# Two cross-attention layers on one core: who writes the second copy of the fifth head group

## The chip, the core and the metric

One core of a Trainium2 chip runs the whole program. The metric is device time in microseconds, the median of several executions. TensorE (PE) multiplies matrices, VectorE (DVE) and ScalarE (ACT) work element by element and can read PSUM, where TensorE puts its results, GpSimd (POOL) works in SBUF, and SyncE (SP) issues most transfers (DMA).

## The reference

Two layers of cross-attention, one behind the other, on 16 sequences of 256 rows with 320 channels, 20 heads of 16 channels each. The context has 256 rows of 512. Its first rows are text (77 in layer 0, 252 in layer 1), the others image tokens (layer 1: the last 4). Shortened, layer 1:

```python
q = heads(hidden_states @ W_q)
k_t, v_t = heads(text_ehs @ W_k), heads(text_ehs @ W_v)
probs_t = softmax(einsum('bhsd,bhtd->bhst', q, k_t) * attn_scale)
text_out = einsum('bhst,bhtd->bhsd', probs_t, v_t)
...
fused = attn_scores + SEM_SCALE * sem
probs_ip = softmax(fused) * spatial_mask[None, None, :, None]
out = text_out + IP_SCALE * einsum('bhsn,bhnd->bhsd', probs_ip, v_ip)
out = out @ W_out + b_out + residual
```

Layer 0 has the same form with another semantic term (`sem` comes from unsplit queries and is shared by all heads) and its own token counts.

## The kernel before

The work is cut into batches b = 0 to 15 and, within each batch, five groups g = 0 to 4 of four heads. A group of one layer is a slot; slot k = 5b + g, 80 slots in layer 0 (`NS`), 80 in layer 1. Each slot forms scores (into PSUM), their row maxima, the exponentials (tile `P`, in SBUF), the products with the values, and then settles them: `settle0` (line 804) or `settle1` (line 985).

**Settling.** The products of a group come with the softmax's denominator as a 17th column, heads along the partitions. VectorE transposes them in blocks of 32x32 (line 807 or 991), takes the reciprocal of the denominator into an unused part of the same PSUM bank (`rz`, line 810 or 1000) and multiplies.

- Layer 0: text and image parts each have a denominator, so VectorE multiplies both (line 813, tile `tmp`, 128x256) and GpSimd adds the two halves into `hsn` (line 814, 128x128).
- Layer 1: VectorE multiplies once, straight into `hsn` (line 1001, 128x128).

**The tile `hsn`** is [128, 3, 8, 2, 16]: three blocks p, 8 row groups, two head groups r, 16 channels. Group g goes to block g // 2, place g % 2. Five groups fill two and a half blocks, and the second place of the third block is filled with a second copy of group 4: it is there so that the output projection's third block can be used for a high and a low part of the same numbers. That copy is made by GpSimd: line 816 in layer 0, line 1005 in layer 1, 128x128 each, once per batch.

**Behind it.** `gather` (line 819) has VectorE transpose the three blocks of `hsn` into `hT` (line 826, 128x256 each); there is one `hsn` and one `hT` for all batches. `finish` (line 830) splits `hT` into high and low parts (`split`, line 589: ScalarE at 593 and 594, GpSimd at 595 and 596) and projects them (TensorE, line 606 and 609). In layer 1, line 1060 (VectorE) adds the image part to `hT` before the split.

**Other work of the same queues.** GpSimd: the multiplies of line 769 in layer 0 and the subtractions of line 925 in layer 1 (128x512, four per slot), splits of context and queries (163, 595, 596), small casts of line 529, which wait for a transfer, the image softmax of layer 1 (1017 to 1050, with the power at 1022). VectorE: the reductions of 740, 741 and 894, which read the scores, the products of line 935, and most PSUM evacuation.

**Order.** Generators are advanced by due times given in slots (`task`, `fill`, `later`; `gather` becomes due 0.45 or 0.4 slots after the fifth group is settled). That gives the program order. In the main loop only TensorE keeps it exactly:

```python
with tc.manual_schedule(engines=PINNED):
    for k in range(2 * NS + 2):
```

`PINNED` holds PE alone, and the context is opened with `schedule_with_timeline_sim=True` (line 1301): a planner sorts the instructions of the other engines at build, by durations that it assumes, and puts in the waits. In the prologue (`begin`) all engines keep the written order. A few instructions are tied behind others of their engine (`anchor`, `queued`).

Of the kernel before, what the change touches and what calls it, by code (L numbers as in the profile page):

```python
# [30 lines left out]
NG = H // 4  # L31
# [18 lines left out]
def xattn2(  # L50
# [27 lines left out]
    nc = tc.nc  # L78
# [31 lines left out]
    def buf(tag, shape, dtype=F32, bufs=1, name=None):  # L110
        if tag in ("wB", "wD", "vr", "raw"):
            return sb.tile(shape, dtype, tag=tag, name=name or tag, bufs=bufs)
        size = 1
        for d in shape[1:]:
            size *= d
        if tag not in slots:
            slots[tag] = [0, dtype] + [const_tile([128, max(size, words.get(tag, 0))], f"{tag}_{i}", dtype) for i in range(bufs)]
        n, kind, *ring = slots[tag]
        assert kind == dtype and len(ring) == bufs, tag
        slots[tag][0] += 1  # L120
        t = ring[n % bufs][: shape[0], :size]
        names = "abcd"[: len(shape) - 1]
        if len(names) > 1:
            t = t.rearrange(f"p ({' '.join(names)}) -> p {' '.join(names)}", **dict(zip(names, shape[1:])))
        return t
# [645 lines left out]
    def attend0(k):  # L771
        b, g = divmod(k, NG)
        v, pv = get("v0", b), own("P")
        for vt in range(3):
            values0(k, pv, v, vt)
        settle0(b, g, pv)
# [27 lines left out]
    def settle0(b, g, pv):  # L804
        hn = hsn
        nt = buf("nt", [128, 2, 8, 32], bufs=2)
        nc.vector.transpose(nt.rearrange("p a f c -> p (a f c)"), pv)  # L807

        rz = pv[:, :16].rearrange("p (a f) -> p a f", a=2)
        nc.vector.reciprocal(rz, nt[:, :, :, 16])  # L810
        nc.vector.tensor_mul(rz[:, 1], rz[:, 1], mk)
        tmp = buf("tmp", [128, 2, 8, 16], bufs=2)
        nc.vector.tensor_mul(tmp, nt[:, :, :, 0:16], rz.unsqueeze(3).to_broadcast([128, 2, 8, 16]))
        nc.gpsimd.tensor_add(hn[:, g // 2, :, g % 2], tmp[:, 0], tmp[:, 1])
        if g == NG - 1:
            nc.gpsimd.tensor_copy(hn[:, 2, :, 1], hn[:, 2, :, 0])
            later(0.45, lambda: gather(0, b))

    def gather(l, b):

        n = l * B + b - 1
        while n >= 0 and ("taken", n) not in results:
            step((f"c{n // B}", n % B))
        hT = buf("hT", [128, 3, S])
        for p in range(3):
            nc.vector.transpose(hT[:, p], hsn[:, p].rearrange("p f r d -> p (f r d)"))
        results["gathered", l, b] = hT
        return hT
# [108 lines left out]
    def attend1(k):  # L937
        pv = bank("P")
        ours, before = k < 2 * NS, k > NS
        if ours:  # L940
            b, g = divmod(k - NS, NG)
            v = get("t1", b)[0]
            for n in range(2):
                for s in range(4):
                    h = V1W * (4 * g + s)
                    mm(  # L946
                        pv[32 * s : 32 * s + 32, :S],
                        v[:, n, h : h + 32],
                        P[k, s // 2][:, n, s % 2],
                        start=n == 0,  # L950
                        stop=n == 1 and not before,
                    )
        if before:
            for n in range(2):
                for s in range(4):
                    mm(pv[32 * s : 32 * s + 32, :S], zone, W[k - 1, s // 2][:, n, s % 2], start=n == 0 and not ours, stop=n == 1)  # L956
        settle1(k, pv)
# [27 lines left out]
    def settle1(k, pv):  # L985
        hn = hsn
        b, g = divmod(k - NS, NG)
        if "na" not in w1:
            w1["na"] = buf("nt", [128, 2, 8, 32], bufs=2, name="na")
        na = w1["na"][:, (k - NS) % 2]  # L990
        nc.vector.transpose(na.rearrange("p f c -> p (f c)"), pv[:, :S])
        if g == 0 and b:
            nc.gpsimd.tensor_copy(norms[b - 1][:, NG, :, 5], na[:, :, 21])
        if b == B:
            return
        if g == 0:
            norms[b] = buf("tmp", [128, NG + 1, 8, 6], bufs=2, name="n1")
        nc.gpsimd.tensor_copy(norms[b][:, g], na[:, :, 16:22])
        rz = pv[:, S : S + 8]
        nc.vector.reciprocal(rz, na[:, :, 16])  # L1000
        nc.vector.tensor_mul(
            hn[:, g // 2, :, g % 2], na[:, :, 0:16], rz.unsqueeze(2).to_broadcast([128, 8, 16])
        )
        if g == NG - 1:
            nc.gpsimd.tensor_copy(hn[:, 2, :, 1], hn[:, 2, :, 0])
            later(0.4, lambda: gather(1, b))

    def image_softmax(b, lo=0, hi=NG):
# [99 lines left out]
    def later(slots, make):  # L1108
        delayed.append((clock[0] + slots, make))
# [196 lines left out]
```

## Time and profile before

| what | value |
|---|---|
| median of 3 runs | 1557.14 us (1554.51 to 1558.83) |
| profiled execution | 1557.65 us |
| its span, first to last instruction | 1555.9 us |
| mean granted TensorE clock | 0.97 |
| layer 0 / layer 1 border | about 751 us |

The profile's page gives busy time per engine over the whole span. Since the two layers have different limits, the views to use are those by window. A row of the groups by line reads: line, engine, operation, output <- inputs, shape, count, then busy time and mean duration of one, then the engine's idle time before it and what ended it. The chain of waits follows the work that ended last back from the end; a piece on it is start, length, engine, tile and line.

### The profile page before, as it was taken

The page shows a single profiled execution, that of the slowest core. Times are in us where ns is not written, and L with a number is a line of the kernel's source. Part 1 is how long each engine was busy: PE and PEld are TensorE (multiplying, and loading weights), DVE is VectorE, ACT ScalarE, POOL GpSimd, SP SyncE. Part 2 cuts the span into 40 slices and gives each one's busy share as a digit, 9 for nine tenths or more (in the row PEclk, how much of TensorE's full clock was granted, in tenths as well). Part 3 has the DMA queues.
Part 4 walks back from the last instruction along what each step waited for, and adds up shares of the span by engine and source line. Part 5 has one row for each costly group of instructions (what it writes and reads, how often), then busy time and mean ns, then how long its engine had stood idle before and what let it go on. Part 6 is the DMA issues. An engine that isn't in the chain of part 4 may idle for free.

```text
span 1555.9 us, 35997 instructions
## 1 busy us (share of the span) xinstructions
PE 1453.4 (93%) x12726; PEld 1169.1 (75%) x12726; DVE 1119.9 (72%) x2544; ACT 891.6 (57%) x2037; POOL 1266.6 (81%) x1357
## 2 busy tenths in 40 slices
PE   6789899989998988888999999999999999999996
PEld 5678787878786877666777777777777778777764
DVE  5466667657666686886777777777778777778784
ACT  5345465645555544554666666666666666666562
POOL 4159698978898886797778988889888988889797
PEclk9899899999999998899999999999999999999998
DMA  6766667666767575666453444444443444433411
GB/s 210 193 185 174 183 183 223 187 205 168 227 168 236 147 222 153 185 179 175 134 158 90 140 112 114 130 119 118 123 134 109 143 110 118 134 114 97 120 32 36
DMA packets 228815, 233.04 MB, mean 150 GB/s; under 512 B 38410, under 2 KB 198508, under 8 KB 228620
## 3 DMA queue, kind: packets, MB, share of 16 engines
q1 hardware_dynamic: 226428, 229.44, 51.8%
q8 instruction: 101, 1.65, 0.5%
q10 hardware_dynamic: 2208, 1.30, 0.3%
q14 instruction: 78, 0.64, 0.1%
HBM read 118.04 MB, written 77.10 MB: 125 GB/s over the span
## 4 chain that ended last, share of the span: by engine, by line
PE 62%; POOL 15%; DMA 8%; DVE 6%; ACT 4%; issue 3%; SPq 2%; ACTq 1%; DVEq 0%; POOLq 0%
PE X L934 13%; PE X L248 12%; PE X L606 6%; POOL wt L925 5%; PE P L796 5%; PE P L946 4%; PE S L739 4%; POOL P L769 4%; PE P L956 3%; PE T L763 3%; PE S L892 3%; PE T L886 3%; DMA qs<-qd 2%; PE X L258 2%; SPq L83 2%
## 5 line engine op out<-in xcount | busy, mean ns | idle before, releaser
L769 POOL TENSOR_TENSOR P<-P,rs 128x512 f32<-128x512 f32 x320 | 408.0, 1299 | 118.0 <-ACT P L766 117.0
L925 POOL TENSOR_TENSOR wt<-P,ctb 128x512 f32<-128x512 f32 x320 | 405.5, 1292 | 61.5 <-ACT ctb L924 61.5
L934 PE MATMUL X<-ctb,gm 128*128 128x512 f32 x1120 | 304.9, 401 | 0.1
L766 ACT ACTIVATE P<-T 128x512 f32<-128x512 f32 x320 | 175.7, 594 | 162.1 <-PE T L763 131.4
L935 DVE TENSOR_TENSOR wt<-X,wt 128x512 f32<-128x512 f32 x320 | 216.9, 683 | 35.3 <-PE X L934 26.8
L934 PEld LDWEIGHTS X<-ctb,gm 128*128 128x128 f32 x1120 | 195.9, 189 | 31.1 <-DVE wt L935 0.6
L906 ACT ACTIVATE P<-T 128x512 f32<-128x512 f32 x320 | 173.6, 595 | 77.5 <-PE T L886 74.6
L924 ACT ACTIVATE ctb<-P 128x512 fp32r<-128x512 f32 x320 | 187.9, 627 | 23.9 <-PE X L934 20.5
L894 DVE TENSOR_REDUCE mn<-S 128x4 fp32r<-128x1008 f32 x160 | 191.6, 1198 | 0.0
L741 DVE TENSOR_REDUCE mn<-S 128x4 fp32r<-128x716 f32 x160 | 142.7, 892 | 0.0
L796 PE MATMUL P<-P,vr 128*32 128x256 f32 x1920 | 132.7, 408 | 5.4 <-POOL P L769 3.5
L739 PE MATMUL S<-ks,qs 125*128 125x256 f32 x640 | 120.8, 313 | 8.2 <-DMA qs<-tph 5.2
L739 PEld LDWEIGHTS S<-ks,qs 125*128 125x128 f32 x640 | 91.2, 200 | 45.8 <-issue 28.4
L763 PE MATMUL T<-qs,ks 127*128 127x256 f32 x640 | 110.6, 295 | 3.4 <-DMA qs<-mt 2.0
L1022 POOL TENSOR_TENSOR r<-u,rs 128x40 f32<-128x40 f32 (+2 forms) x17 | 108.7, 6395 | 4.4 <-DVE u L1019 4.4
L740 DVE TENSOR_REDUCE mn<-S 128x4 fp32r<-128x308 f32 x160 | 74.7, 467 | 33.7 <-PE S L739 32.6
L763 PEld LDWEIGHTS T<-qs,ks 127*128 127x128 f32 x640 | 93.1, 199 | 6.5 <-ACT P L766 2.6
L807 DVE STREAM_TRANSPOSE nt<-P 128x512 f32<-128x512 f32 x80 | 57.1, 714 | 55.5 <-PE P L796 54.9
L796 PEld LDWEIGHTS P<-P,vr 128*32 128x32 f32 x1920 | 57.6, 114 | 49.8 <-issue 10.6
L606 PE MATMUL X<-ho,wF 128*128 128x256 f32 x512 | 75.7, 289 | 19.3 <-POOL ho L596 11.1
L606 PE MATMUL X<-hq,wE 128*128 128x256 f32 x512 | 82.3, 301 | 11.1 <-POOL hq L595 5.8
L606 PEld LDWEIGHTS X<-ho,wF 128*128 128x128 f32 x512 | 67.1, 190 | 28.7 <-POOL ho L596 12.1
(234 smaller groups left out, 3042.7 us busy)
## 6 DMA issues: line engine op xcount, KB each, us to landing
qd<-q SPq DMA_DIRECT2D x96, 256.0 KB
qs<-tph SPq DMA_DIRECT2D x64, 308.0 KB
rawc<-in_cT_dram SPq DMA_DIRECT2D x60, 256.0 KB
qs<-qd SPq DMA_DIRECT2D x80, 192.0 KB
ks<-kd SPq DMA_DIRECT2D x80, 192.0 KB
ks<-kd SPq DMA_DIRECT2D x160, 96.0 KB
qs<-qd SPq DMA_DIRECT2D x160, 96.0 KB
kd<-kst SPq DMA_DIRECT2D x57, 256.0 KB
```

The costliest lines, as they stand in the source:

```text
L248: last = mm(out, lhs(a, k), rhs(b, k), start=i == 0, stop=i == len(terms) - 1)
L606: mm(pp, w(s, k, m), a[:, t], start=i == 0, stop=i == len(terms) - 1)
L739: mm(sp[:, h], Q[: XROW + T0, h, t * 128 : (t + 1) * 128], K[: XROW + T0, h], start=True, stop=True)
L763: mm(st[p][:, j], K[:KS0, 2 * p + j, t * 128 : (t + 1) * 128], Q[:KS0, 2 * p + j], start=True, stop=True)
L766: exp = anchor(nc.scalar.activation(pt, st[p], AF.Exp, scale=SCALE))
L769: anchor(nc.gpsimd.tensor_mul(pt, pt, rs[:, t : t + 1].to_broadcast([128, 2, S])))
L796: mm(pv[32 * s : 32 * s + 32, o : o + S], v[:, vt, h : h + 32], P[k, s // 2][:, t, s % 2], start=vt < 2, stop=vt != 1,)
L894: anchor(nc.vector.tensor_reduce(maxes[k + 2][:, t], sp[:, :, :T1], axis=AX.X, op=ALU.max))
L924: nc.scalar.activation(R[k, u][:, t], P[k, u][:, t], AF.Copy, scale=0.5)
L925: anchor(nc.gpsimd.tensor_sub(W[k, u][:, t], P[k, u][:, t], f(R[k, u][:, t])))
L934: mm(yp, gm[:, gb], R[k, u][:, kt], start=i == 0, stop=i == len(blocks[n]) - 1)
L935: nc.vector.tensor_mul(W[k, u][:, n], yp, W[k, u][:, n])
```

## The change

In both layers the fifth group (g = 4) is written to both places of the third block by one instruction. The inputs are read twice by an access pattern that repeats the 16 channels (a broadcast over the place r), so that the output is the whole block, 128x256 and contiguous. The two GpSimd copies go. Groups 0 to 3 stay as they were.

```diff
-        nc.gpsimd.tensor_add(hn[:, g // 2, :, g % 2], tmp[:, 0], tmp[:, 1])
-        if g == NG - 1:
-            nc.gpsimd.tensor_copy(hn[:, 2, :, 1], hn[:, 2, :, 0])
+        if g < NG - 1:
+            nc.gpsimd.tensor_add(hn[:, g // 2, :, g % 2], tmp[:, 0], tmp[:, 1])
+        else:
+            one, two = [tmp[:, i].unsqueeze(2).to_broadcast([128, 8, 2, 16]) for i in range(2)]
+            nc.gpsimd.tensor_add(hn[:, 2], one, two)
             later(0.45, lambda: gather(0, b))
...
-        nc.vector.tensor_mul(
-            hn[:, g // 2, :, g % 2], na[:, :, 0:16], rz.unsqueeze(2).to_broadcast([128, 8, 16])
-        )
-        if g == NG - 1:
-            nc.gpsimd.tensor_copy(hn[:, 2, :, 1], hn[:, 2, :, 0])
+        if g < NG - 1:
+            nc.vector.tensor_mul(
+                hn[:, g // 2, :, g % 2], na[:, :, 0:16], rz.unsqueeze(2).to_broadcast([128, 8, 16])
+            )
+        else:
+            one, two = [t.to_broadcast([128, 8, 2, 16]) for t in (na[:, :, 0:16].unsqueeze(2), rz.unsqueeze(2).unsqueeze(3))]
+            nc.vector.tensor_mul(hn[:, 2], one, two)
             later(0.4, lambda: gather(1, b))
```

In layer 0 the work stays on GpSimd, in layer 1 the second half moves from GpSimd to VectorE, and the third transpose of line 826 then follows its producer on the same engine.

## The prediction

> **What bounds the kernel now.** I read the page's totals first, then the busy time of each engine in windows cut at the stage borders (layer 0 up to about 751 us, layer 1 behind it, the last batch from 1490).
>
> ```profile
> span 1555.9 us, 35997 instructions
> PE 1453.4 (93%) x12726; PEld 1169.1 (75%) x12726; DVE 1119.9 (72%) x2544; ACT 891.6 (57%) x2037; POOL 1266.6 (81%) x1357
> core 0: us, PE busy (x) PEld busy (x) DVE busy (x) ACT busy (x) POOL busy (x), PEclk, DMA share, GB/s
> 206.00:528.00 322.00, 303.11 (x2806) 257.28 (x2803) 215.48 (x522) 179.80 (x432) 277.34 (x277) 0.98 0.68 197
> 528.00:751.00 223.00, 195.66 (x1704) 159.07 (x1703) 168.39 (x373) 118.44 (x281) 181.37 (x191) 0.92 0.64 181
> 755.00:1150.00 395.00, 390.94 (x3454) 304.49 (x3454) 306.45 (x669) 250.68 (x554) 333.14 (x376) 1.00 0.44 122
> 1150.00:1490.00 340.00, 338.13 (x3021) 262.14 (x3020) 266.60 (x585) 215.35 (x473) 299.81 (x326) 1.00 0.41 116
> 1490.00:1556.00 66.00, 51.04 (x389) 35.41 (x387) 40.16 (x87) 24.66 (x48) 51.41 (x57) 0.91 0.12 37
> ```
>
> The reader is to see two different kernels. In layer 1 TensorE is idle for 4.06 us of 395 and 1.87 us of 340, at a granted clock of 1.00: whatever VectorE or GpSimd saves there meets an engine that hardly waits. In layer 0 TensorE is idle for 18.9 us of 322 and 27.3 us of 223, and in the last 66 us for 15.0 us; there GpSimd, VectorE, ScalarE and transfers take turns on the path, so there an order can gain or lose. GpSimd is busiest after TensorE, 81% of the span, and the change is mostly about its queue.
>
> **The rows of the changed work**, from the groups by line with shapes kept apart (the last columns are busy us, mean ns of one, idle before).
>
> ```profile
> L814 POOL TENSOR_TENSOR hsn<-tmp 128x128 f32<-128x128 f32 x80 | 37.8, 472 | 3.7 <-DVE tmp L813 3.7
> L816 POOL COPY hsn<-hsn 128x128 f32<-128x128 f32 x16 | 4.7, 296 | 0.0
> L1005 POOL COPY hsn<-hsn 128x128 f32<-128x128 f32 x16 | 4.7, 291 | 0.0
> L998 POOL COPY tmp<-nt 128x48 f32<-128x48 f32 x80 | 18.1, 226 | 2.4 <-DVE nt L991 2.4
> L596 POOL TENSOR_TENSOR ho<-hT,ho 128x256 fp32r<-128x256 f32 x32 | 23.6, 737 | 2.5 <-ACT ho L594 2.5
> L1050 POOL TENSOR_TENSOR rs<-rs,kb 128x384 f32<-128x384 f32 x16 | 16.3, 1018 | 0.0
> L1001 DVE TENSOR_TENSOR hsn<-nt,P 128x128 f32<-128x128 f32 x80 | 22.9, 286 | 2.3
> L813 DVE TENSOR_TENSOR tmp<-nt,P 128x256 f32<-128x256 f32 x80 | 33.3, 416 | 2.0
> L935 DVE TENSOR_TENSOR wt<-X,wt 128x512 f32<-128x512 f32 x320 | 216.9, 683 | 35.3 <-PE X L934 26.8 <-POOL wt L925 4.2
> L163 DVE TENSOR_TENSOR wB<-rawc,wB 128x512 fp32r<-128x512 f32 x3 | 4.0, 1335 | 0.0
> ```
>
> **Layer 0, GpSimd.** One copy per batch goes: 16 of 296 ns, 4.7 us. The add of the fifth group grows from 128 to 256 elements a partition, 16 times. The trace has no such add; the nearest row, the 128x256 add at line 596, takes 737 ns. Bounds: 472 ns, if the second read of the same 16 values costs nothing, and 1018 ns, the 128x384 row. I take 740, so 16 x (740 - 472) = 4.3 us come back, net -0.4 us of GpSimd work, between -4.7 and +4.0. No DMA, no queue and no other engine's instruction is moved by the text of the change. The third transpose (line 826, VectorE) waited for the copy and will wait for the longer add.
>
> [...]
>
> From the rows: the copy costs (291 - 226) / 80 = 0.8 ns an element, the add (737 - 472) / 128 = 2.1 ns, but the copy also carries about 187 ns that don't depend on its size (291 - 128 x 0.81). 268 ns added against 296 ns removed is a wash.
>
> What of that is on the path? The chain that ended last, in order of time, around the fifth group of the third batch, and the last place in layer 0 where it holds the copy:
>
> ```profile
> 212.86 0.42 POOL hsn L814
> 213.28 2.49 POOL P L769 x2
> 215.77 0.05 POOL hsn L816
> ...
> 672.52 0.23 POOL hsn L816
> ```
>
> Add and copy stand in one unbroken GpSimd stretch, with two multiplies (line 769) between. The sum of the stretch falls by 28 ns. The chain holds the copy four times in layer 0, from 215.77 to 672.52 us, which gives -0.1 us. Elsewhere the copy fell where GpSimd was off the path, while the longer add holds up the two multiplies behind it by 0.27 us. If that hit the path in all 16 batches it would be +4.3 us. I take -0.1 us for layer 0.
>
> **Layer 1, GpSimd and VectorE.** 16 copies of 291 ns go from GpSimd: 4.7 us. The VectorE multiply of line 1001 grows from 128 to 256 elements for the fifth group. Its nearest row is line 813: the same engine, one input in SBUF, the other a value in PSUM spread over 16 elements, 256 of them, 416 ns. Bounds: 286 ns (nothing added) and 683 ns (the 128x512 row). I take 416: 16 x 130 ns = +2.1 us, between 0 and +6.4. Behind this multiply on VectorE stand the copy of line 861 and the reduction of line 894, which free the score bank; they come 0.13 us later once per batch. TensorE's weight loads that wait for such things find them early: layer 1 has under 6 us of TensorE idleness in 735 us in all.
>
> ```profile
> L1001 DVE TENSOR_TENSOR hsn<-nt,P x80: 268/287/291, 753.8 to 1526.0; 128x128 f32<-128x128 f32 x80
> ```
>
> [...]
>
> The gain of layer 1 is a wait. The last transpose of a batch needs the copy, and the copy stood behind other GpSimd work. The waits (us in total, times, longest) and the one place where that chain decided, first on the chain, then on the timeline:
>
> ```profile
> DVE hT L826 <- POOL hsn L1005: 7.7, 7, 1.7
> PE X L609 <- DVE wt L935: 1.1, 1, 1.1
> ...
> 794.85 3.05 DMA kd<-kst
> ...
> 798.05 0.19 POOL kst L529
> 798.24 0.22 POOL u L1017
> 798.47 0.24 POOL hsn L1005
> ...
> 798.73 0.45 DVE hT L826
> ```
>
> ```profile
> 798.56 1.15 ACT L924 ACTIVATE ctb<-P 128x512 fp32r<-128x512 f32 x2
> 799.10 1.25 DVE L935 TENSOR_TENSOR wt<-X,wt 128x512 f32<-128x512 f32 x2
> 800.41 0.86 PE L609 MATMUL X<-hq,wE 128*128 128x256 f32 x5 [1.07 <-DVE wt L935]
> ```
>
> After the change the transpose follows the multiply on its own engine and no longer waits for a transfer through GpSimd. The 7.7 us of VectorE idleness goes; but TensorE idled only in the first of the seven, 1.07 us before line 609. That is what I count: -1.1 us (what is late next there is the bank behind line 935, 1.25 us of VectorE work that can now start 1.65 us sooner). The six others, under a TensorE that never stopped, count nothing; if that cover were gone they would give at most the other 6 us.
>
> At the end GpSimd is on the path and the last copy with it:
>
> ```profile
> 1528.40 0.23 POOL hsn L1005
> 1528.63 0.43 POOL rs L1042
> ```
>
> -0.23 us. **Sum:** -0.1 - 1.1 - 0.2 = -1.4 us. The profiled execution took 1557.65 us (span 1555.9 and 1.75 around it), so 1556.2; the median of the runs, 1557.14, lies 0.5 lower, so 1555.7.
>
> **The rivals.** All share one fact: only TensorE's order is written out in the main loop. For the other queues a planner sorts the instructions at build, by durations that it assumes; a copy less and a longer multiply per batch can sort them anew, far from the edit.
>
> 1. A sorting that helps. Layer 0 has the room: GpSimd holds up the output projection.
>
> ```profile
> PE X L606 <- POOL ho L596: 11.1, 5, 2.8
> ```
>
> Half of these 11.1 us gone with the GpSimd queue less cut up would be -5.5 us: 1550.2. For it: 46 us of TensorE idleness in two windows of layer 0. Against it: net GpSimd work there falls by only 0.4 us.
>
> 2. A sorting that hurts, on the other side of zero. Place: layer 0 between 528 and 751 us, where next-layer weights and the stores and reloads of queries share SyncE's queue, and TensorE already idles 27.3 us. Price: one more such trip laid bare on the path, as the chain has them already:
>
> ```profile
> 406.45 6.25 DMA qs<-qd
> 743.75 4.61 DMA qd<-q
> ```
>
> +6.25 gives 1562.0, +4.61 gives 1560.3. It decides as soon as a store or reload is sorted behind a GpSimd or VectorE step that ends later than TensorE's use of it. Against it: the edit moves any instruction by some 0.3 us only, and the layer 1 part has so little slack in DMA (share 0.4) that it can hardly occur there.
>
> 3. Nothing arrives: the copy's time is only moved into the longer instructions and the 1.1 us at 800 us is taken by the next late thing (the rounding on ScalarE, line 924, started at 798.56): 1557.1.
>
> **How the numbers follow.** Chances: my forecast 0.55, helpful sorting 0.18, harmful sorting 0.17, nothing 0.10. 0.3% is 4.7 us, about what a measurement of this kernel can tell from no change: faster means below 1552.5, slower above 1561.8. Faster: 0.16 of the first rival's 0.18 and 0.05 of the forecast, where small gains of order add up (the 4.7 us of copies in layer 1, or the 6 us of waits): 0.21. Slower: 0.14 of the harmful sorting and 0.04 of the forecast, where the longer add meets the path in most batches (+4.3 us) and something else besides: 0.18. Same: 0.61. The range takes in both sortings: 1549 to 1563.
>
> **What would show it.** Right: no copy of line 816 or 1005 is left, the fifth group's add takes about 740 ns and its multiply about 416 ns, VectorE's idle time before the transpose no longer names that copy, TensorE does not idle before line 609 at 800 us, and layer 1 from 850 to 1490 us lasts as long as before. Wrong: an add beyond 1 us or a multiply beyond 0.7 us (sizes); TensorE's idleness in layer 0 changed by more than 5 us with these sizes right (sorting); or a shorter layer 1, which would say that TensorE was waiting there after all.

## The result

The changed kernel takes 1540.06 us in the median of 5 runs (1533.3 to 1543.37), against 1557.14 us before. The ratio is 0.9902, 95% interval 0.9879 to 0.9924: about 1% faster, some 15 us. The forecast was 1555.7 us with a range from 1549 to 1563; the time lies below it.

The profiled execution of the changed kernel is its fastest run (1533.3 us, span 1531.5), so its trace shows some 7 us more than the median does. The page's totals, and the busy time by window, cut at the same stages as before, with the columns of the prediction's rows:

```profile
span 1531.5 us, 36088 instructions
PE 1439.7 (94%) x12726; PEld 1162.6 (76%) x12726; DVE 1116.6 (73%) x2544; ACT 891.0 (58%) x2037; POOL 1263.5 (83%) x1325
200.00:507.00 307.00, 294.27 (x2768) 251.33 (x2768) 211.08 (x513) 176.77 (x424) 272.62 (x265) 0.99 0.71 204
507.00:726.00 219.00, 190.77 (x1703) 157.21 (x1701) 165.35 (x373) 118.34 (x281) 181.84 (x186) 0.95 0.65 184
730.00:1125.00 395.00, 391.98 (x3461) 305.33 (x3460) 307.49 (x670) 250.59 (x555) 332.40 (x369) 1.00 0.44 122
```

GpSimd's total fell by 3.1 us. TensorE ran the same 12726 matmuls, yet its busy time fell by 13.7 us, and its idle time (span less busy) from 102.5 to 91.8 us. The same work in less busy time went with a higher granted clock: 0.970 over the span before, 0.982 after.

Where did the time go? The last VectorE transpose of layer 0 (line 807 in both) and the first of layer 1 (line 991 before, 993 after) date the two layers. First the kernel before, then after; the two times behind the durations are the first and the last start:

```profile
L807 DVE STREAM_TRANSPOSE nt<-P x80: 674/717/719, 81.5 to 746.5; 128x512 f32<-128x512 f32 x80
L991 DVE STREAM_TRANSPOSE nt<-P x81: 405/450/451, 753.1 to 1533.3; 128x256 f32<-128x256 f32 x81
```

```profile
L807 DVE STREAM_TRANSPOSE nt<-P x80: 669/718/720, 78.0 to 721.3; 128x512 f32<-128x512 f32 x80
L993 DVE STREAM_TRANSPOSE nt<-P x81: 406/450/451, 727.7 to 1508.7; 128x256 f32<-128x256 f32 x81
```

Layer 0 ends 25.2 us sooner. Of these, 3.5 us lie ahead of its first transpose (81.5 against 78.0 us). In the traces of the three other kernels below that keep such a copy on GpSimd it starts at 77.9 to 79.1 us, so most of the 3.5 us belong to this one execution and not to the edit. Layer 1, from its first transpose to the end of the span, takes 803.8 us against 802.8: nothing was gained there. The forecast had it the other way round, -0.1 us for layer 0.

**What became of the copy's place.** Here is a batch of layer 0 before, in lines picked from the timeline (start, length, engine, line; idle before and its releaser in brackets):

```profile
330.83 0.46 POOL L814 TENSOR_TENSOR hsn<-tmp 128x128 f32<-128x128 f32 x1
...
332.34 2.54 POOL L769 TENSOR_TENSOR P<-P,rs 128x512 f32<-128x512 f32 x2 [0.34 <-ACT P L766]
334.81 0.31 POOL L816 COPY hsn<-hsn 128x128 f32<-128x128 f32 x1
335.06 2.56 POOL L769 TENSOR_TENSOR P<-P,rs 128x512 f32<-128x512 f32 x2
...
335.79 0.42 DVE L813 TENSOR_TENSOR tmp<-nt,P 128x256 f32<-128x256 f32 x1
336.85 0.53 DVE L269 TENSOR_TENSOR X<-X,kst 64x358 f32<-64x358 f32 x1 [0.65 <-ACT both L268]
...
338.56 2.49 POOL L769 TENSOR_TENSOR P<-P,rs 128x512 f32<-128x512 f32 x2 [0.54 <-ACT P L766]
339.26 0.43 DVE L826 STREAM_TRANSPOSE hT<-hsn 128x256 f32<-128x256 f32 x1
339.73 0.51 ACT L594 ACTIVATE ho<-hT,tmask 128x256 fp32r<-128x256 f32 x1 [0.76 <-DVE hT L826]
341.02 0.72 POOL L596 TENSOR_TENSOR ho<-hT,ho 128x256 fp32r<-128x256 f32 x1
341.79 0.51 PE L606 MATMUL X<-ho,wF 128*128 128x256 f32 x2 [2.77 <-POOL ho L596]
342.23 2.25 PE L796 MATMUL P<-P,vr 128*32 128x256 f32 x24
```

And the same batch after the change, picked in the same way:

```profile
318.96 0.75 POOL L818 TENSOR_TENSOR hsn<-tmp 128x256 f32<-128x256 f32 x1
...
320.49 5.19 POOL L769 TENSOR_TENSOR P<-P,rs 128x512 f32<-128x512 f32 x4 [0.25 <-ACT P L766]
323.43 0.43 DVE L828 STREAM_TRANSPOSE hT<-hsn 128x256 f32<-128x256 f32 x1
324.86 0.51 ACT L594 ACTIVATE ho<-hT,tmask 128x256 fp32r<-128x256 f32 x1
325.64 0.45 POOL L815 TENSOR_TENSOR hsn<-tmp 128x128 f32<-128x128 f32 x1
326.05 0.72 POOL L596 TENSOR_TENSOR ho<-hT,ho 128x256 fp32r<-128x256 f32 x1
326.59 1.20 PE L606 MATMUL X<-ho,wF 128*128 128x256 f32 x8 [0.88 <-ACT mt L749]
327.72 1.50 PE L796 MATMUL P<-P,vr 128*32 128x256 f32 x24
```

Before, two multiplies stood between the add and the copy. The transpose came 8.4 us after the add's start (339.26 - 330.83), against 4.5 us after the change. By then two more multiplies were in GpSimd's queue ahead of the low split (line 596): six multiplies between add and split instead of four. The hardware did not hold the transpose back for the copy, which had ended at 335.12 us: VectorE, without a wait for it, did eight other instructions first, two of which are shown, against three between the add's end and the transpose after the change. That is the order of its queue, fixed at build. That the planner set the transpose later because the copy came later in its plan is inferred from kernels with and without this dependency (below); its plan itself is in no trace. TensorE had begun the output projection and stood still for 2.77 us inside it. Behind the stall the 24 value products took 2.25 us instead of 1.50: the same matmuls at a lower clock. The windows behind the stall, before, and behind the same projection, after, show it in the column PEclk (the one with 0.58, then 1.00):

```profile
342.20:346.30 4.10, 4.10 (x34) 2.75 (x34) 1.84 (x4) 0.15 (x1) 0.00 (x0) 0.58 0.08 21
```

```profile
327.70:331.20 3.50, 3.50 (x45) 2.72 (x45) 2.54 (x6) 0.48 (x1) 1.94 (x2) 1.00 0.76 213
```

Cut from one fifth-group transpose to the next, that batch took 41.6 us before and 37.1 us after, with 349 matmuls in each:

```profile
325.10:366.70 41.60, 38.35 (x349) 32.77 (x349) 27.46 (x66) 21.43 (x51) 29.31 (x31) 0.95 0.60 174
407.30:445.00 37.70, 36.42 (x349) 31.41 (x349) 27.18 (x66) 21.33 (x51) 30.23 (x32) 1.00 0.69 197
```

```profile
313.60:350.70 37.10, 36.22 (x349) 31.42 (x350) 27.25 (x67) 21.18 (x51) 30.28 (x31) 1.00 0.73 206
```

The second row of the kernel before is a batch without the stall: it is as quick there as after the change. So the stall costs 3.9 to 4.5 us by these rows; against the batch after the change it is 2.4 us of standing still (TensorE idle 3.25 us against 0.88 us) and 2.1 us of slower matmuls (38.35 against 36.22 us busy). The trace of before holds three such stalls of 2.76 to 2.77 us, at 180, 342 and 503 us, and two smaller ones at 588 and 678 us (0.68 and 2.16 us); after the change only two smaller ones are left. The row of these waits, before and after:

```profile
PE X L606 <- POOL ho L596: 11.1, 5, 2.8
```

```profile
PE X L606 <- POOL ho L596: 2.4, 2, 1.8
```

### The profile page after: what moved, and what is told of

It is laid out like the page before. It is cut to its first block, busy times and chain, and to the rows that moved or that the text cites. A ratio compares the mean times of both kernels' runs of the same rounds, so it can differ in the third digit from the quotient of the medians.

```text
span 1531.5 us, 36088 instructions
## 1 busy us (share of the span) xinstructions
PE 1439.7 (94%) x12726; PEld 1162.6 (76%) x12726; DVE 1116.6 (73%) x2544; ACT 891.0 (58%) x2037; POOL 1263.5 (83%) x1325
## 4 chain that ended last, share of the span: by engine, by line
PE 69%; POOL 11%; DMA 8%; DVE 5%; ACT 3%; issue 2%; SPq 1%; ACTq 1%; POOLq 0%; DVEq 0%
PE X L936 14%; PE X L248 13%; PE X L606 6%; PE P L796 5%; PE P L948 4%; POOL wt L927 4%; PE S L739 4%; PE P L958 4%; PE T L763 3%; PE T L888 3%; PE S L894 3%; DMA ks<-M 2%; POOL P L769 2%; PE X L258 2%; PE X L609 2%
## 5 line engine op out<-in xcount | busy, mean ns | idle before, releaser
L796 PE MATMUL P<-P,vr 128*32 128x256 f32 x1920 | 125.5, 391 | 4.7 <-POOL P L769 3.3
L739 PE MATMUL S<-ks,qs 125*128 125x256 f32 x640 | 117.2, 306 | 6.0 <-DMA qs<-tph 3.4
L948 PE MATMUL P<-P,v1t 128*32 128x256 f32 x1280 | 85.9, 386 | 0.0
```

The costliest lines, as they stand in the source:

```text
L739: mm(sp[:, h], Q[: XROW + T0, h, t * 128 : (t + 1) * 128], K[: XROW + T0, h], start=True, stop=True)
L796: mm(pv[32 * s : 32 * s + 32, o : o + S], v[:, vt, h : h + 32], P[k, s // 2][:, t, s % 2], start=vt < 2, stop=vt != 1,)
```

## The experiments

Three theories stood against each other. **Place**: the copy, queued two multiplies behind the add, made the third transpose, the low split and TensorE's projection late. **Work**: GpSimd has less to do. **Chance**: any edit sorts the planner's queues anew, and this draw was a good one.

**Each half of the change alone.** Layer 0's half, without the edit of lines 1001 to 1005 (shortened; the lines are those of the change):

```diff
...
+            nc.gpsimd.tensor_add(hn[:, 2], one, two)
-            nc.gpsimd.tensor_copy(hn[:, 2, :, 1], hn[:, 2, :, 0])
             later(0.45, lambda: gather(0, b))
```

> Layer 0's half of the change alone (layer 1 keeps its GpSimd copy). Place theory (in layer 0 the copy was queued two multiplies behind the add, so the third transpose, the low split of line 596 and TensorE's output projection came late; the merged add ends that): all of the gain, ratio 0.988 to 0.993, TensorE's waits for the low split fall from 11.1 us to 3 us or less. Work theory (GpSimd has 4.7 us fewer copies in layer 1 and 0.4 us less in layer 0): no gain, ratio 0.998 to 1.002. Chance theory (any edit sorts the planner's queues anew): anything from 0.985 to 1.01.

Measured: 1538.81 us, ratio 0.9898 (0.9863 to 0.9933): all of the gain. TensorE's wait for the low split fell to 2.4 us. Layer 1's half, without the edit of lines 814 to 816 (shortened in the same way):

```diff
...
+            nc.vector.tensor_mul(hn[:, 2], one, two)
-            nc.gpsimd.tensor_copy(hn[:, 2, :, 1], hn[:, 2, :, 0])
             later(0.4, lambda: gather(1, b))
```

> Layer 1's half alone (layer 0 keeps add and copy). Place theory: layer 0 as before, and layer 1 is paced by TensorE, so ratio 0.998 to 1.001 with at most 1.3 us gained (the stall at the first layer 1 batch and the copy in the last one). Work theory: 4 to 5 us gained, 0.997 or less. Chance theory: anything from 0.985 to 1.01.

Measured: 1553.12 us, ratio 0.9981 (0.9962 to 1.0000). The low split's waits stayed at 11.1 us in 5. The best value is a gain of some 2 to 3 us, but the interval reaches to none. The traces limit it: from its first transpose (line 991 or its place in the edited kernel) to the end of the span, layer 1 takes 800.9 to 803.8 us in the six traces with the merged multiply (median 803.1 us) and 802.1 to 807.4 us in the six without it (median 803.9 us). So layer 1 gave about 1 us or nothing. The gain of the whole is layer 0's.

**The dependency put back, and the same work without it.** To the changed kernel:

```diff
             nc.gpsimd.tensor_add(hn[:, 2], one, two)
+            nc.gpsimd.tensor_copy(hn[:, 2, :, 1], hn[:, 2, :, 0])
```

> The whole change, and behind layer 0's merged add a GpSimd copy that writes the second place once more with the same values, so that the third transpose waits for a copy again. GpSimd work: 4.7 us more than after the change. Place theory: the copy is queued behind multiplies again and the gain of layer 0 is gone, 1553 to 1560 us, ratio 0.997 to 1.002, waits of TensorE for the low split 8 us or more. Work theory: 1540 plus at most 5, about 1545. Chance theory: anything.

Measured: 1564.74 us, ratio 1.0055 (1.0037 to 1.0073): slower than before by 0.5%, which is more than was expected, because the stall is back and more often. The lines show it first in the view of line 606 (what TensorE idled for there, us and times), then in one batch of its timeline:

```profile
  POOL ho L596: 20.0, 7
```

```profile
326.81 0.74 POOL L818 TENSOR_TENSOR hsn<-tmp 128x256 f32<-128x256 f32 x1
...
328.36 2.53 POOL L769 TENSOR_TENSOR P<-P,rs 128x512 f32<-128x512 f32 x2 [0.27 <-ACT P L766]
330.84 0.29 POOL L819 COPY hsn<-hsn 128x128 f32<-128x128 f32 x1
331.08 2.55 POOL L769 TENSOR_TENSOR P<-P,rs 128x512 f32<-128x512 f32 x2
...
334.59 2.49 POOL L769 TENSOR_TENSOR P<-P,rs 128x512 f32<-128x512 f32 x2 [0.54 <-ACT P L766]
...
337.04 0.71 POOL L596 TENSOR_TENSOR ho<-hT,ho 128x256 fp32r<-128x256 f32 x1
```

Again the copy stands behind two multiplies and the split behind six. Now the same copy into a tile that nobody reads (`junk`, 128x128, whose allocation is left out here):

```diff
             nc.gpsimd.tensor_add(hn[:, 2], one, two)
+            nc.gpsimd.tensor_copy(junk, hn[:, 2, :, 0])
```

> The whole change, and behind layer 0's merged add a GpSimd copy of the same size into a tile that nobody reads. Same GpSimd work as the kernel with the repeated copy, but nothing waits for it. Place theory: as after the change, 1537 to 1543 us, ratio 0.987 to 0.993. Work theory: about 1545, as with the repeated copy. Chance theory: anything, and no reason that it should differ from the repeated copy in this direction.

Measured: 1537.32 us, ratio 0.9875 (0.9830 to 0.9921), one wait of 1.7 us for the low split. Same work on GpSimd, 27 us apart. That fells the work theory, and the chance theory would have had to guess both directions.

**A shove somewhere else.** To the kernel before, a copy behind the second group's add, into a tile `junk` again:

```diff
+        if g == 1:
+            nc.gpsimd.tensor_copy(junk, hn[:, 0, :, 0])
```

> The kernel before, with one more GpSimd copy per batch of layer 0, of the same size, behind the add of the second group, into a tile that nobody reads: a shove to the planner's sorting that has nothing to do with the fifth group. In the order that it is built with, six multiplies stand between the fifth group's add and the low split (line 596) in five batches of layer 0, against three in the kernel before. Place theory: about 4.2 us for each such batch (2.77 us wait of TensorE and the lower clock behind it), so 2 x 4.2 slower than before, 1560 to 1567 us, five waits of 2.8 us. Work theory: 16 x 0.29 us more GpSimd work, at most 4.7 us slower. Chance theory: any time from 1535 to 1575, with no tie to these places.

Measured: 1560.54 us, ratio 1.0022 (0.9995 to 1.0048). The trace has four stalls of 2.77 us and one of 3.76 us, six waits and 17.2 us in all. The count came as the built order had it; the time grew by 4.6 us in the median, not by 8.4, and its interval still touches no change, so the time by itself shows nothing. Its trace is clearer: the four batches with the stall of 2.77 us took 41.3 to 42.5 us, the tenth, without it, 37.1 us (cut as above). The expectation counted two more such stalls; there is one more of them, and the fifth, of 3.76 us, falls in a batch that stood for 0.68 us before.

**Three other ways to get rid of the place.** Each changes only layer 0 of the kernel before. First a second add in place of the copy: it depends on `tmp`, as the first add does, and not on the first add:

```diff
-            nc.gpsimd.tensor_copy(hn[:, 2, :, 1], hn[:, 2, :, 0])
+            nc.gpsimd.tensor_add(hn[:, 2, :, 1], tmp[:, 0], tmp[:, 1])
```

> The kernel before, where in layer 0 the copy is replaced by a second GpSimd add of the same two halves of tmp into the second place: more GpSimd work than before (about 16 x 0.18 us), layer 1 as before, but the second instruction does not wait for the first. No batch has six multiplies between the first add and the low split. Place theory: the gain of layer 0 without any merged instruction, ratio 0.987 to 0.993. Work theory: at least as slow as before, 1.000 to 1.003. Chance theory: anything.

Measured: 1539.08 us, ratio 0.9899 (0.9864 to 0.9934). More work on GpSimd than before, no merged instruction, and the whole gain. Next, the copy on ScalarE:

```diff
-            nc.gpsimd.tensor_copy(hn[:, 2, :, 1], hn[:, 2, :, 0])
+            nc.scalar.copy(hn[:, 2, :, 1], hn[:, 2, :, 0])
```

> The kernel before, where layer 0's copy is made by ScalarE in place of GpSimd (layer 1 as before). The copy leaves the queue in which the multiplies stand. No batch has six multiplies between add and low split. Place theory: 0.987 to 0.994, perhaps a little dearer than the merged add, since ScalarE's exponentials come 16 times later by a copy. Work theory: GpSimd is 4.7 us lighter, at most 4.7 us faster, 0.997. Chance theory: anything.

Measured: 1538.83 us, ratio 0.9901 (0.9866 to 0.9936). And on VectorE:

```diff
-            nc.gpsimd.tensor_copy(hn[:, 2, :, 1], hn[:, 2, :, 0])
+            nc.vector.tensor_copy(hn[:, 2, :, 1], hn[:, 2, :, 0])
```

> The kernel before, where layer 0's copy is made by VectorE, which also makes the transpose behind it (layer 1 as before). No batch has six multiplies between add and low split, but five have four multiplies and two context splits, as four batches of the kernel before have. Place theory: those did not stall TensorE before, so 0.987 to 0.994 here too; if it comes out at 0.997 or more, the theory counts the wrong places. Work theory: at most 4.7 us faster. Chance theory: anything.

Measured: 1536.11 us, ratio 0.9881 (0.9845 to 0.9918). In both, a single wait of 0.7 us for the low split. The last tells that the context splits do not take the place of multiplies: five batches with four multiplies and two context splits stalled nothing. Six multiplies stalled TensorE by 2.76 us or more in every batch that had them, in all the traces; they are not the only way to it, since the wait of 2.16 us at 678 us in the kernel before has four.

**The best of these beside the change.** VectorE's copy in layer 0 with layer 1's merged multiply, and the changed kernel again. To the change, the first without any edit:

```diff
-            one, two = [tmp[:, i].unsqueeze(2).to_broadcast([128, 8, 2, 16]) for i in range(2)]
-            nc.gpsimd.tensor_add(hn[:, 2], one, two)
+            nc.gpsimd.tensor_add(hn[:, 2, :, 0], tmp[:, 0], tmp[:, 1])
+            nc.vector.tensor_copy(hn[:, 2, :, 1], hn[:, 2, :, 0])
```

> The changed kernel once more, beside the next one on the same chip. 0.988 to 0.992.

> The changed kernel with layer 0's copy on VectorE in place of the merged add, and layer 1's merged multiply kept. Place theory: neither of the two has a batch with six multiplies between add and low split, so they are equal within what can be told, 0.986 to 0.992 both; the fifth group's add is 0.27 us shorter on GpSimd here, 16 times, which is worth at most 4 us if GpSimd were the bound of layer 0. Chance theory: they may differ either way.

Measured: 1538.13 us, ratio 0.9888 (0.9857 to 0.9919) for the change, 1544.22 us, ratio 0.9910 (0.9874 to 0.9946) for the other. The two can't be told apart, and nothing here is shown to beat the change.

All kernels in the order of what TensorE waited for the low split. The last two columns are of the trace: the time from the first to the eleventh fifth-group transpose of line 807, which is ten batches, and the stalls of 2.76 to 2.77 us in it.

| kernel | copy's way in layer 0 | waits, us (times) | ratio | ten batches, us | stalls in them |
|---|---|---|---|---|---|
| copy on ScalarE | ScalarE | 0.7 (1) | 0.9901 | 387.3 | 0 |
| copy on VectorE | VectorE | 0.7 (1) | 0.9881 | 389.0 | 0 |
| copy on VectorE, layer 1's half | VectorE | 0.7 (1) | 0.9910 | 389.2 | 0 |
| unread copy added | merged add | 1.7 (1) | 0.9875 | 388.6 | 0 |
| two adds | second add | 1.7 (1) | 0.9899 | 389.1 | 0 |
| layer 0's half | merged add | 2.4 (2) | 0.9898 | 388.2 | 0 |
| the change, twice | merged add | 2.4 (2) | 0.9902, 0.9888 | 388.8, 388.8 | 0 |
| before | GpSimd copy | 11.1 (5) | 1 | 406.3 | 3 |
| layer 1's half | GpSimd copy | 11.1 (5) | 0.9981 | 402.3 | 3 |
| shove at the second group | GpSimd copy | 17.2 (6) | 1.0022 | 407.8 | 4 |
| copy put back | merged add, then copy | 20.0 (7) | 1.0055 | 411.1 | 5 |

The kernels fall into two groups by these waits, and the ratio goes with the group, not with the number of GpSimd's instructions; inside the first group the ratios can't be told apart. All the stalls of the last column lie in the second, fourth, sixth, eighth or tenth of the ten batches. Over the twelve traces such a batch took 41.2 to 42.5 us with the stall (15 of them) and 36.7 to 37.8 us without (45): about 4.2 us a stall. The chance theory is not needed for any row. That the planner sorts anew is true in each of them, but what it sorts worse or better that matters is this one chain.

## Why the prediction was wrong, step by step

**The durations were right.** The merged add, taken at 740 ns, has a mean of 736 ns; the merged multiply, taken at 416 ns, has a median of 421 ns:

```profile
L818 POOL TENSOR_TENSOR hsn<-tmp 128x256 f32<-128x256 f32 x16 | 11.8, 736 | 0.0
L1009 DVE TENSOR_TENSOR hsn<-nt,P 128x256 f32<-128x256 f32 x16 | 6.7, 421 | 0.6
```

The merged multiply took 420 to 422 ns in all 16 batches. The weighing of the copy against the longer add was right too, a wash: the merged add takes 276 ns more than the 460 ns of the 128x128 add after the change, against the 296 ns of the copy. One row is not what it seems. The 1335 ns of the subtraction of line 163 are a mean of three, 680, 1540 and 1784 ns; the two long ones ran while GpSimd did multiplies of line 769, the short one while it did none. (And a DMA share of 0.4, in the second rival, is much slack, not little.)

**Layer 1 was right in the main.** Under a TensorE that hardly waits, the 4.7 us of copies and the 7.7 us of VectorE idleness bought nothing to be seen. The 1.07 us of TensorE idleness before line 609 at 800 us is gone from the waits of after, as said, and so is VectorE's wait for the copy. The last batches stayed about as they were: TensorE's waits for the transpose of the image weights are 6.2 us before and 5.2 us after, first before, then after:

```profile
PE X L1059 <- DVE rs L1049: 6.2, 2, 4.6
```

```profile
PE X L1063 <- DVE rs L1053: 5.2, 2, 3.9
```

**The step that failed is layer 0, "I take -0.1 us for layer 0".** The prediction costed the copy by its duration, 296 ns taken out against 268 ns put in, and by the pieces that the chain that ended last gives to it, which are 0.05 to 0.23 us. Both measure how long the copy runs. What it cost was where it stood: a result of which the first half was ready at 331 us was not complete until 335 us, and everything behind it, transpose, cast, split, projection, was built later with it. The term put at -0.1 us measured 12.6 us in the trace of before, three stalls of about 4.2 us; layer 0's half alone took 1538.81 us against 1555.49 us beside it. The prediction says that the third transpose "waited for the copy and will wait for the longer add" and does not follow that sentence further. It saw two multiplies between add and copy in the chain and drew from them only the sum of the stretch. VectorE did not idle before that transpose, which hid the delay: its queue held other work until then, so the lateness showed up three instructions on, under another name, as TensorE waiting for the low split. The prediction's own second sign of being wrong came about: with the sizes right, TensorE's idleness fell by 10.7 us, nearly all of it in layer 0.

**The rival that came nearest** was the first one, which quotes that very row, 11.1 us in 5. It had the right wait and the wrong reason (a planner's luck, "half of these 11.1 us"), a chance of 0.18 and 1550.2 us. The change takes away 8.7 us of the 11.1 (2.4 are left), and the clock behind each long stall raises its price from 2.8 us to about 4.2. Three of these stalls make 12.6 us of the 15 to 17 measured.

What makes up the other 3 to 5 us stays open. The ten batches with the stalls took 402.3 and 406.3 us in the two traces that have three of them, and 387.3 to 389.2 us in the eight that have none, which is 13 to 19 us; so what the stalls leave over is no more than the two traces of the same layer 0 differ by. The rival that the sorting would hurt, 1562 us, did not come about in layer 0.

## What to carry to other kernels

The price of a small instruction that depends on the one just before it in its own queue need not be its duration: a scheduler may put long, ready work between the two, and then the delay of its last reader counts. Here a copy of 0.31 us stood behind two multiplies that took 2.54 us together, and the batches with the stall took about 4.2 us more. So follow the result of each removed instruction through every reader up to the engine that bounds the stage, and look in the list of waits for the far end of that chain, not for the instruction's own name. If the second result can be made from the same inputs as the first, the dependency goes even when the work grows.

## What was not expected of the hardware

A long stall of TensorE was paid twice in these traces, by the wait and by the clock behind it. After waits of 2.76 to 3.63 us the granted clock was 0.50 to 0.64 over the next 4.1 or 4.2 us in eight places, in the kernel before and the one with the copy put back (0.58 in the window shown above), and a wait of 2.16 us at 678 us in the kernel before was followed by 0.50 and 0.78; after a wait of 1.76 us at 653 us in the changed kernel it stayed at 1.00. The rows behind these last two waits, before and after:

```profile
677.80:679.80 2.00, 2.00 (x18) 1.09 (x22) 2.00 (x1) 0.00 (x0) 2.00 (x2) 0.50 0.22 58
679.80:682.00 2.20, 2.20 (x25) 1.25 (x17) 2.20 (x8) 0.00 (x0) 0.22 (x1) 0.78 0.15 29
```

```profile
653.30:655.30 2.00, 2.00 (x28) 1.11 (x29) 2.00 (x3) 0.00 (x0) 2.00 (x3) 1.00 0.68 180
```

The border is not sharp. Of all the waits of TensorE between 100 and 1480 us that had at least 4 us of full clock before them, in the twelve traces, the 51 of 2 us or more were all followed by a lower clock (0.50 to 0.73 over the next 4.1 us), whatever TensorE had waited for; of the 30 between 1.5 and 2 us, 11 were not. In the kernel with the unread copy a wait of 1.72 us at the same place of the program was followed by 0.65:

```profile
661.10:665.20 4.10, 4.06 (x33) 2.64 (x34) 2.17 (x6) 0.00 (x0) 3.12 (x3) 0.65 0.61 151
```

In three of the eight places the granted clock was 0.50 over all of the 4.1 or 4.2 us. A change that removes a wait of TensorE like these, 2.77 us long, should therefore be priced, in this kernel, at about one and a half times the wait: a batch with the stall took about 4.2 us more.
